# A two-layer graph network kernel: LayerNorm statistics from the adding instruction and from ScalarE, later reloads of dense tiles, another order of the last products

## The chip, the cores and the metric

The kernel runs on one core of one Trainium2 chip. The metric is the device time of one execution in microseconds, lower is better; a time given for a kernel is the median of its runs.

## The reference

The input is a matrix x of 2500 nodes by 1024 features (f32), 80,000 edges (src, dst, weight), two 1024 x 1024 weight matrices and a bias. Two residual layers follow each other, each on the ReLU of a LayerNorm without scale and shift:

```python
h = jnp.maximum(_layernorm(x, axis=-1), 0.0)
# layer 0: messages from src, weighted, summed at dst
support = jnp.matmul(h, W0)
x1 = x + segment_sum(support[src] * edge_weight[:, None], dst, 2500)
h = jnp.maximum(_layernorm(x1, axis=-1), 0.0)
# layer 1: a normalized graph convolution with self loops, row = src, col = dst
hid = jnp.einsum('nd,od->no', h, W1) + b
norm = deg_inv_sqrt[row] * deg_inv_sqrt[col]
out = x1 + segment_sum(norm[:, None] * hid[col], row, 2500)
```

The LayerNorm between them, of x1, is the one that the change touches: for every row its mean m, its variance v, and max((x1 - m) / sqrt(v + eps), 0).

## The kernel before

Nodes are cut into 20 tiles of 128 rows. The edges come sorted by dst, and tile t has TILE_BLOCKS[t] blocks of 128 edges (146, 62, 48, 41 for tiles 0 to 3, then 36 down to 10).

**First stage.** For each tile: the statistics of x, a transposed and normalized tile, its product with W0 (L282), and a store of the rows into `support` in DRAM. Beside that, edges are counted: for each block two one-hot matrices (VectorE, L446 and L448) are multiplied (L450), and VectorE adds the result to `counts[t]` (L458). For tiles 0 to 3, the "dense" ones (DENSE = 4), weighted sums are built as well (L455, L462, L466), so that their aggregation is a plain matrix product later.

**Middle stage.** The other sixteen, the "thin" tiles, are aggregated block by block in `gathered` (L587): an indirect DMA on the POOL queue brings 128 rows of `support` into `msg` (L592, eight buffers), VectorE makes a one-hot matrix `oh_r` (L596), ScalarE makes `hi`, the weighted message rounded to fp32r (L598), VectorE the remainder `lo` (L600), each with two buffers, and TensorE multiplies the one-hot matrix with both (four matmuls, L604). The dense tiles go in pairs, (3, 2) and then (1, 0), through `multiplied` (L613): for each half of the columns, 20 steps of two products `dense` x `support` (L632), whose messages come by a plain DMA on the POOL queue (L625). At the end of a half VectorE adds x (L640) and SP stores both tiles' halves to `x1_d` in DRAM (L642).

**`finish` (L552)** takes a tile on. A thin tile loads x, adds the sums from PSUM (L562, VectorE) and stores x1 to `x1_d` on SP's queue (L563). A dense tile is read back from `x1_d` on SP's queue (L557), since its halves came at different times. Then comes `normed` (L138): bn_stats on both halves and bn_aggr (VectorE, L133 and L135), the square root on ScalarE (L141), the reciprocal and the shift on VectorE (L142, L143), and the Relu with scale and shift on ScalarE (L145), which gives `hn`. `transposed` (L542) turns it on TensorE (L546) with copies by ScalarE (L547), and `second_rows` (L571) multiplies it with W1 (L577, 32 hardware matmuls per tile), adds the bias in two halves (L581, VectorE) and stores `hid` (L584, SP). `hn` and `hid` share a name and so the same two buffers of the pool `work`.

**What sets the order.** A list `plan` of 458 steps (L654 to L669) says for each step whether a dense or a thin piece is next. Beside it, the loop at L695 takes pieces of products at a `rate`, one part of a tile's preparation (`preparing`) each time that `parts` has reached 1, and as many counting groups as three planner clocks (TensorE, VectorE, ScalarE) allow: every generator yields what it takes of each (for `normed` 2.2 us of VectorE and 1.5 of ScalarE), and counting goes on until VectorE's clock has passed TensorE's (L519 to L523), or while more is left than a line that falls over the plan allows. A preparation begins only when fewer than two products are left over (L714). Tiles that still wait at the end are worked off at L732 to L737: first the preparations, then the products. The framework may move instructions of one engine against this order where its own timing model finds the engine free; `order_behind` (L274) adds an edge, without a semaphore, that keeps an instruction behind another one in that order.

**Second stage.** From L758 on, `hid` is read back, scaled and split into hi and lo (L764 to L769), and the second aggregation is 20 row tiles x 20 tiles of matmuls with the transposed counts (L794), finished by an add and a store (L782, L784). The buffers of this stage take the place of those of the middle stage, whose last user is the last product.

The two places that the change rewrites in the loop and after it:

```python
        if parts == 1 and preparing is None and len(products_left) < 2 and (waiting or stored):
            preparing = waiting.pop(0) if waiting else finish(stored.pop(0))
...
    for rest in [preparing] * (preparing is not None) + waiting:
        for _ in rest:
            pass
    for rest in products_left:
        for _ in rest:
            pass
```

Of the kernel before, what the change touches and what calls it, by code (L numbers as in the profile page):

```python
# [9 lines left out]
F32 = mybir.dt.float32  # L10
# [5 lines left out]
AF = mybir.ActivationFunctionType  # L16
ALU = mybir.AluOpType
DVE = mybir.EngineType.DVE

P = 128  # L20
# [12 lines left out]
DENSE = 4  # L33
# [14 lines left out]
def direct(  # L48
# [26 lines left out]
    nc = tc.nc  # L75
    N, D = x.shape
# [13 lines left out]
    def rows(t):  # L90
        return min(P, N - t * P)
# [17 lines left out]
    eps = keep.tile([P, 1], F32, name="eps")  # L109
# [9 lines left out]
    lay = first.enter_context(tc.tile_pool(name="lay", bufs=1))  # L119
    work = first.enter_context(tc.tile_pool(name="work", bufs=2))  # L120
# [9 lines left out]
    def moments(xt, pool):  # L130
        stats = pool.tile([P, 2, 6], F32, name="stats")
        for h in range(2):
            nc.vector.bn_stats(stats[:, h, :], xt[:, h * H:(h + 1) * H])  # L133
        mv = pool.tile([P, 2], F32, name="mv")
        nc.vector.bn_aggr(mv, stats)  # L135
        return mv

    def normed(xt, pool):  # L138
        mv = moments(xt, pool)
        rstd = pool.tile([P, 2], F32, name="rstd")  # L140
        nc.scalar.activation(rstd[:, 0:1], mv[:, 1:2], AF.Sqrt, bias=eps)  # L141
        nc.vector.reciprocal(rstd[:, 0:1], rstd[:, 0:1])  # L142
        nc.vector.scalar_tensor_tensor(rstd[:, 1:2], mv[:, 0:1], -1.0, rstd[:, 0:1], op0=ALU.mult, op1=ALU.mult)  # L143
        hn = pool.tile([P, D], F32, name="hn")
        nc.scalar.activation(hn, xt, AF.Relu, scale=rstd[:, 0:1], bias=rstd[:, 1:2])  # L145
        return hn

    def load_rows(t, pool):
        xt = pool.tile([P, D], F32, name="xt")
        if rows(t) < P:  # L150
            nc.vector.memset(xt, 0.0)
        nc.sync.dma_start(xt[:rows(t), :], x[t * P:t * P + rows(t), :])
        return xt
# [92 lines left out]
    bias = lay.tile([P, D], F32, name="bias")  # L246
# [16 lines left out]
    last_pe = None  # L263
# [3 lines left out]
    def on_pe(i):  # L267
        nonlocal last_pe
        last_pe = i
        if len(fences) >= BEHIND and fences[-BEHIND] is not None:  # L270
            order_behind(i, fences[-BEHIND])
        return i

    def order_behind(i, other):  # L274
        tc.add_manual_dep(i.ins, other.ins.name,
                          mybir.DependencyInfo(mybir.DependencyClass.NoSync, mybir.DependencyReason.SCHED_ONLY),
                          reason="order of the steps")
# [60 lines left out]
    for a in range(0, NBP, 4 * P):  # L338
# [5 lines left out]
                                       op0=ALU.max, op1=ALU.min)  # L344
# [10 lines left out]
    for t in range(NT):  # L355
# [3 lines left out]
        for a, n, m, g0 in ((a, n, g, g0), (a + n * g, int((b - a) % g > 0), (b - a) % g, g0 + n)):  # L359
            if n:  # L360
                v = first_row[:, a:a + n * m].rearrange("p (n g) -> p n g", g=m)
                nc.vector.tensor_copy(base_i[0:1, g0:g0 + n], v[0:1, :, 0])
                for q in range(1, m) if t < 2 else ():
# [9 lines left out]
                                   accum_out=placed[:, 0:1])  # L373
# [24 lines left out]
    rest = wgt_p[:, :KD]  # L398
    for i in range(2):
# [3 lines left out]
        rest = wpart[:, 2]  # L403
# [121 lines left out]
    def count_all(t):  # L525
        for queue in to_count:
            while any(g[0] == t for g in queue):
                count_next(queue)
# [13 lines left out]
    def transposed(v, into):  # L542
        for k0 in range(0, KC, 4):
            pT = psum.tile([P, 4, P], F32, name="pT")
            for k in range(4):
                nc.tensor.transpose(pT[:, k, :], v[:, (k0 + k) * P:(k0 + k + 1) * P], ident)  # L546
            nc.scalar.copy(into[:, k0:k0 + 4, :], pT)  # L547
            yield 0.7, 0.0, 0.6
# [3 lines left out]
    def finish(t, sums=None):  # L552


        if sums is None:
            xt = work.tile([P, D], F32, name="xt")
            nc.sync.dma_start(xt, x1_d[t])  # L557
            for _ in range(3):
                yield 0.0, 0.0, 0.0
        else:  # L560
            xt = load_rows(t, work)
            nc.vector.tensor_add(xt, sums.rearrange("p h d -> p (h d)"), xt)  # L562
            nc.sync.dma_start(x1_d[t], xt)  # L563
            yield 0.0, 1.25, 0.0
        hn = normed(xt, work)
        yield 0.0, 2.2, 1.5
        vT = work.tile([P, KC, P], F32, name="vT")
        yield from transposed(hn, vT)
        products_left.append(second_rows(t, vT))
# [39 lines left out]
            yield 0.92, 1.47, 1.16  # L609

    last_load = None

    def multiplied(ts):  # L613


        nonlocal last_load, pending
        for t in ts:
            count_all(t)
        for h in range(2):
            sums = psum.tile([P, 2, H], F32, name="mm")  # L620
            cols = slice(h * H, (h + 1) * H)
            for k0 in range(0, NT, 2):
                msg = gpool.tile([P, 2, H], F32, name="msg", bufs=8)
                if rows(k0 + 1) == P:
                    last_load = nc.gpsimd.dma_start(  # L625
                        msg, support[k0 * P:(k0 + 2) * P, cols].rearrange("(k p) d -> p k d", p=P))
                else:
                    for k in (k0, k0 + 1):
                        last_load = nc.gpsimd.dma_start(msg[:rows(k), k - k0], support[k * P:k * P + rows(k), cols])
                for k in (k0, k0 + 1):  # L630
                    for i, t in enumerate(ts):
                        m = nc.tensor.matmul(sums[:, i, :], dense[t][:rows(k), k, :], msg[:rows(k), k - k0],  # L632
                                             start=(k == 0), stop=(k == NT - 1))
                        if i == 0:
                            on_pe(m)
                    if k == NT - 1:
                        xt = work.tile([P, 2, H], F32, name="xt")
                        for i, t in enumerate(ts):
                            nc.sync.dma_start(xt[:, i], x[t * P:(t + 1) * P, cols])
                        nc.vector.tensor_add(xt, sums, xt)  # L640
                        for i, t in enumerate(ts):
                            nc.sync.dma_start(x1_d[t][:, cols], xt[:, i])  # L642
                        takes(v=1.25)
                        if h == 1:
                            stored.extend(ts)
                            pending += PIECES * len(ts)
                    yield 1.75, 0.0, 0.0

# [22 lines left out]
    waiting, stored, products_left = [], [], []  # L671
# [16 lines left out]
    def rows_of(tiles):  # L688
        for i in range(0, DENSE, 2):
            yield from multiplied(tiles[i:i + 2])  # L690
# [3 lines left out]
    preparing = None  # L694
    for i, is_dense in enumerate(plan):  # L695
        if stretch[i]:
            rate = min(pending - (3 if i + stretch[i] < len(plan) else 0), 14) / stretch[i]
        took = next(kinds[is_dense])
        if i == OPENING:
            for k in range(KC):  # L700
                w1_sb.append(wpool.tile([P, D], F32, name=f"w{k}"))
        if i >= OPENING and (i - OPENING) < KC:
            order_behind(nc.sync.dma_start(w1_sb[i - OPENING], w1t[(i - OPENING) * P:(i - OPENING + 1) * P, :]),
                         last_load)
        if i == OPENING + KC:
            nc.sync.dma_start(bias, b1.rearrange("(o d) -> o d", o=1).to_broadcast([P, D]))
        pieces = min(pieces + rate, 2.0)
        while pieces >= 1 and products_left:
            takes(*next(products_left[0]))
            pieces, pending = pieces - 1, pending - 1  # L710
            if pending % PIECES == 0:
                assert next(products_left.pop(0), None) is None
        parts = min(parts + 0.7, 1.0)
        if parts == 1 and preparing is None and len(products_left) < 2 and (waiting or stored):  # L714
            preparing = waiting.pop(0) if waiting else finish(stored.pop(0))
        if parts == 1 and preparing is not None:
            part = next(preparing, None)
            if part is None:
                preparing = None
            else:  # L720
                takes(*part)
                parts = 0.0
        count(*took, least=todo * (1 - 1.05 * (i + 1) / len(plan)))
# [5 lines left out]
            count_next(queue)  # L729
    store_counts(late=False)  # L730
    assert not stored
    for rest in [preparing] * (preparing is not None) + waiting:  # L732
        for _ in rest:
            pass
    for rest in products_left:
        for _ in rest:
            pass  # L737


    nc.vector.tensor_reduce(deg, total, axis=mybir.AxisListType.X, op=ALU.add)  # L740
# [17 lines left out]
    lay = ctx.enter_context(tc.tile_pool(name="lay2", bufs=1, reuse_waits="tile"))  # L758
    work = ctx.enter_context(tc.tile_pool(name="work2", bufs=2, reuse_waits="tile"))
    psum = ctx.enter_context(tc.tile_pool(name="psum2", bufs=2, space=bass.MemoryType.PSUM, reuse_waits="tile"))  # L760
    his, los = {}, {}
    for t in ORDER:
# [6 lines left out]
                                       op0=ALU.mult, op1=ALU.subtract)  # L769
# [370 lines left out]
```

## Time and profile before

| what | value |
|---|---|
| median of 3 runs | 1740.54 us (1735.30 to 1742.44) |
| the profiled execution | 1733.96 us |
| its span, first to last instruction | 1732.0 us |
| granted TensorE clock | 0.988 |
| TensorE matmul busy | 1654.1 us (96%) |
| VectorE busy | 1200.3 us (69%) |
| ScalarE busy | 907.9 us (52%) |
| HBM read and written | 282.41 MB and 54.56 MB |

The profile is one execution. Its page lists busy time by engine and the span in 40 slices; a group is all instructions of one line, engine and operation with the mean duration of one (in ns) and the idle time of the engine just before them, by what ended it. The waits list says who waited for whom, with the total, the number and the longest. The chain of waits follows the work back from the last instruction; each of its lines has start, length and what ran. The ends of matmuls are modelled, and they are pipelined, so a busy TensorE isn't one at its peak. A matmul of f32 data over 512 columns is two hardware instructions.

By stretch: until about 480 us the first stage runs, from 480 to 1346 the middle stage, and from there the second aggregation. The last counting matmuls run near 1130 us. The last dense pair is added at 1192.2 us, the last thin tile at 1316.9 us.

### The profile page before, as it was taken

The numbers are of one execution on the slowest core, as the hardware profiler recorded it, in microseconds if no ns is written. First come the engines' busy times: TensorE is split into PE (matmuls) and PEld (weight loads), VectorE is DVE, ScalarE is ACT, GpSimd is POOL, SyncE is SP. The second block draws the span as 40 slices with busy tenths as digits, with TensorE's granted clock in tenths as the row PEclk, the third lists the DMA queues.
The fourth block names the chain that finished last, engine by engine and source line by source line (L and its number), as shares of the span: only waits on it lengthen the run. The fifth ranks groups of instructions, "written<-read, shape, count | busy, mean of one in ns | idle before, by whom it ended". The sixth has DMA issues, their size and how long they took to land. (4 is left out here: it accounts for less than half of the span.)

```text
span 1732.0 us, 21214 instructions
## 1 busy us (share of the span) xinstructions
PE 1654.1 (96%) x6506; PEld 1030.8 (60%) x6506; DVE 1200.3 (69%) x3051; ACT 907.9 (52%) x1476; POOL 525.6 (30%) x501
## 2 busy tenths in 40 slices
PE   6999999999999999999999999998999899999997
PEld 2466555554445555655555555654564678888886
DVE  5788888888889999999999999996772510000000
ACT  3399999982236765665555556664553421111110
POOL 3000000000057776775555556664530000000000
PEclk9999999999999999999999999999999999999999
DMA  7512212123399999998988899898875663433320
GB/s 249 188 62 65 89 53 60 54 68 92 79 364 330 384 317 323 331 362 281 308 286 282 282 322 331 318 333 297 264 265 134 210 164 91 107 79 105 93 65 32
DMA packets 213584, 351.57 MB, mean 203 GB/s; under 512 B 115354, under 2 KB 134820, under 8 KB 213462
## 3 DMA queue, kind: packets, MB, share of 16 engines
q0 software_dynamic: 60592, 219.74, 36.2%
q1 hardware_dynamic: 152870, 130.39, 24.8%
q8 instruction: 54, 0.88, 0.2%
q14 instruction: 68, 0.56, 0.1%
HBM read 282.41 MB, written 54.56 MB: 195 GB/s over the span
## 5 line engine op out<-in xcount | busy, mean ns | idle before, releaser
L598 ACT ACTIVATE hi<-msg,wgt_p 128x1024 fp32r<-128x1024 f32 x378 | 428.6, 1149 | 280.6 <-PE mm L604 180.4
L592 POOL DMA_INDIRECT msg<-support,src_p x378 | 478.0, 1265 | 293.6 <-DVE oh_r L596 90.0
L600 DVE SCALAR_TENSOR_TENSOR lo<-msg,wgt_p,hi 128x1024 fp32r<-128x1024 f32 x378 | 480.1, 1277 | 36.7 <-ACT hi L598 21.1
L604 PE MATMUL mm<-lo,oh_r 128*128 128x512 f32 x756 | 309.8, 491 | 13.2 <-DVE lo L600 13.0
L282 PE MATMUL mm<-w,hT 128*128 128x512 f32 x640 | 318.4, 609 | 2.4 <-ACT hT L174 2.4
L577 PE MATMUL pT<-w,vT 128*128 128x512 f32 x640 | 312.4, 597 | 0.0
L604 PE MATMUL mm<-hi,oh_r 128*128 128x512 f32 x756 | 273.5, 442 | 0.7 <-ACT hi L598 0.7
L455 ACT ACTIVATE wl<-oh_low,wpart 128x128 bf16<-128x128 bf16 x891 | 262.2, 420 | 0.0
L794 PE MATMUL mm<-hi,bT 128*128 128x512 f32 (+1 forms) x800 | 247.6, 392 | 4.6 <-ACT bT L776 2.0
L794 PE MATMUL mm<-lo,bT 128*128 128x512 f32 (+1 forms) x800 | 247.7, 392 | 3.3 <-DVE lo L768 3.3
L782 DVE SCALAR_TENSOR_TENSOR rows<-mm,dis,rows 128x1024 f32<-128x1024 f32 x20 | 25.7, 1283 | 307.9 <-PE mm L794 307.8
L604 PEld LDWEIGHTS mm<-lo,oh_r 128*128 128x128 f32 x756 | 137.9, 189 | 129.3 <-DVE lo L600 51.1
L448 DVE TENSOR_SCALAR oh_key<-iota,key 128x200 bf16<-128x200 f16 (+12 forms) x675 | 194.4, 290 | 5.0 <-PE cb L462 4.9
L776 ACT CAST bT<-cT 128x2560 fp32r<-128x2560 f16 x20 | 46.6, 2335 | 261.0 <-PE mm L794 257.7
L604 PEld LDWEIGHTS mm<-hi,oh_r 128*128 128x128 f32 x756 | 139.3, 189 | 64.2 <-issue 30.2
L794 PEld LDWEIGHTS mm<-hi,bT 128*128 128x128 f32 (+1 forms) x800 | 150.4, 189 | 37.9 <-ACT hi L766 3.1
L794 PEld LDWEIGHTS mm<-lo,bT 128*128 128x128 f32 (+1 forms) x800 | 150.0, 188 | 38.3 <-DVE lo L768 7.0
L458 DVE TENSOR_TENSOR counts<-cb,counts 128x200 f32 (+13 forms) x296 | 138.5, 469 | 48.0 <-PE cb L450 41.2
L446 DVE TENSOR_SCALAR oh_low<-iota,low 128x128 bf16<-128x128 f16 x675 | 167.2, 251 | 1.4 <-ACT wl L455 1.2
L632 PE MATMUL mm<-msg,dense 128*128 128x512 f32 (+1 forms) x320 | 157.1, 601 | 10.2 <-DMA msg<-support 10.2
L577 PEld LDWEIGHTS pT<-w,vT 128*128 128x128 f32 x640 | 120.9, 191 | 72.6 <-issue 55.5
L282 PEld LDWEIGHTS mm<-w,hT 128*128 128x128 f32 x640 | 109.1, 195 | 65.4 <-issue 59.2
(144 smaller groups left out, 1177.5 us busy)
## 6 DMA issues: line engine op xcount, KB each, us to landing
msg<-support POOLq DMA_DIRECT2D x36, 512.0 KB, 6.8
xt<-in_x SPq DMA_DIRECT2D x34, 512.0 KB, 7.3
cnat<-counts SPq DMA_DIRECT2D x20, 640.0 KB, 5.4
hid_d<-hn SPq DMA_DIRECT2D x20, 512.0 KB, 6.5
rows<-hid_d SPq DMA_DIRECT2D x20, 512.0 KB, 4.4
rows<-x_d SPq DMA_DIRECT2D x20, 512.0 KB, 3.8
hT<-in_xT SPq DMA_DIRECT2D x19, 512.0 KB, 3.7
support<-row SPq DMA_DIRECT2D x19, 512.0 KB, 2.9
```

The costliest lines, as they stand in the source:

```text
L282: on_pe(nc.tensor.matmul(mm[:, h, :], vT[:, k, :], ws[k][:, h * H:(h + 1) * H], start=(k == 0), stop=(k == KC - 1)))
L446: nc.vector.tensor_scalar(oh_low, iota16[:, :P], low[:, k:k + 1], None, op0=ALU.is_equal)
L448: nc.vector.tensor_scalar(oh_key[:, :NT * w], iota16[:, :NT * w], key[:, k:k + 1], None, op0=ALU.is_equal)
L455: nc.scalar.activation(wl[:, i, :], oh_low, AF.Copy, scale=wpart[:, i, k:k + 1])
L458: nc.vector.tensor_tensor(to, cb[:, :NT * w].rearrange("p (t w) -> p t w", w=w), to, op=ALU.add)
L577: on_pe(nc.tensor.matmul(mm, vT[:, k, :], w1_sb[k][:, h * H:(h + 1) * H], start=(k == 0), stop=(k == KC - 1)))
L592: nc.gpsimd.indirect_dma_start(out=msg, out_offset=None, in_=support, in_offset=bass.IndirectOffsetOnAxis(ap=src_p[:, k:k + 1], axis=0))
L598: nc.scalar.activation(hi, msg, AF.Copy, scale=wgt_p[:, k:k + 1])
L600: nc.vector.scalar_tensor_tensor(lo, msg, wgt_p[:, k:k + 1], hi.bitcast(F32), op0=ALU.mult, op1=ALU.subtract)
L604: i = nc.tensor.matmul(sums[:, h, :], oh, v[:, h * H:(h + 1) * H], start=(j == 0 and v is hi), stop=(j == n - 1 and v is lo))
L632: m = nc.tensor.matmul(sums[:, i, :], dense[t][:rows(k), k, :], msg[:rows(k), k - k0], start=(k == 0), stop=(k == NT - 1))
L794: nc.tensor.matmul(mm[:, h, :], bT[:rows(k), k, :], v[:rows(k), h * H:(h + 1) * H], start=(k == ORDER[0] and v is his[k]), stop=(k == ORDE ...
```

## The change

In `normed`, bn_stats and bn_aggr are gone. The row sum `sum_` comes in as an argument, VectorE turns it into minus the mean, ScalarE takes Square of x1 minus the mean with its sum as accumulator output (its elements go into `hn`, which Relu overwrites later), and Sqrt takes scale 1/D. For a thin tile the row sum is the accumulator output of the add, now a scalar_tensor_tensor; for a dense tile the add at the end of each half is one scalar_tensor_tensor per tile with an accumulator output into `halves[t]`, and the two are added in `finish`. For a dense tile Square is ordered behind the last TensorE instruction written before it. The planner is told 0.4 us of VectorE and 2.7 of ScalarE for `normed`. An entry of `stored` becomes ready after four steps. At the end, products left over are worked off before the remaining preparations, and once more after them.

```diff
--- before.py
+++ after.py
@@ -135,14 +135,19 @@
         nc.vector.bn_aggr(mv, stats)
         return mv
 
-    def normed(xt, pool):
-        mv = moments(xt, pool)
+    def normed(xt, sum_, pool, behind):
+
+        hn = pool.tile([P, D], F32, name="hn")
+        mean = pool.tile([P, 2], F32, name="mean")
+        nc.vector.tensor_scalar(mean[:, 0:1], sum_, -1.0 / D, None, op0=ALU.mult)
         rstd = pool.tile([P, 2], F32, name="rstd")
-        nc.scalar.activation(rstd[:, 0:1], mv[:, 1:2], AF.Sqrt, bias=eps)
+        i = nc.scalar.activation(hn, xt, AF.Square, bias=mean[:, 0:1], accum_out=rstd[:, 1:2])
+        if behind is not None:
+            order_behind(i, behind)
+        nc.scalar.activation(rstd[:, 0:1], rstd[:, 1:2], AF.Sqrt, scale=1.0 / D, bias=eps)
         nc.vector.reciprocal(rstd[:, 0:1], rstd[:, 0:1])
-        nc.vector.scalar_tensor_tensor(rstd[:, 1:2], mv[:, 0:1], -1.0, rstd[:, 0:1], op0=ALU.mult, op1=ALU.mult)
-        hn = pool.tile([P, D], F32, name="hn")
-        nc.scalar.activation(hn, xt, AF.Relu, scale=rstd[:, 0:1], bias=rstd[:, 1:2])
+        nc.vector.tensor_mul(mean[:, 1:2], mean[:, 0:1], rstd[:, 0:1])
+        nc.scalar.activation(hn, xt, AF.Relu, scale=rstd[:, 0:1], bias=mean[:, 1:2])
         return hn
 
     def load_rows(t, pool):
@@ -555,15 +560,19 @@
         if sums is None:
             xt = work.tile([P, D], F32, name="xt")
             nc.sync.dma_start(xt, x1_d[t])
+            sum_ = work.tile([P, 1], F32, name="sum_")
+            nc.vector.tensor_add(sum_, halves[t][:, 0:1], halves[t][:, 1:2])
             for _ in range(3):
                 yield 0.0, 0.0, 0.0
         else:
             xt = load_rows(t, work)
-            nc.vector.tensor_add(xt, sums.rearrange("p h d -> p (h d)"), xt)
+            sum_ = work.tile([P, 1], F32, name="sum_")
+            nc.vector.scalar_tensor_tensor(xt, sums.rearrange("p h d -> p (h d)"), 1.0, xt,
+                                           op0=ALU.mult, op1=ALU.add, accum_out=sum_)
             nc.sync.dma_start(x1_d[t], xt)
             yield 0.0, 1.25, 0.0
-        hn = normed(xt, work)
-        yield 0.0, 2.2, 1.5
+        hn = normed(xt, sum_, work, last_pe if sums is None else None)
+        yield 0.0, 0.4, 2.7
         vT = work.tile([P, KC, P], F32, name="vT")
         yield from transposed(hn, vT)
         products_left.append(second_rows(t, vT))
@@ -609,6 +618,7 @@
             yield 0.92, 1.47, 1.16
 
     last_load = None
+    halves = {t: lay.tile([P, 2], F32, name=f"halves{t}") for t in range(DENSE)}
 
     def multiplied(ts):
 
@@ -637,12 +647,13 @@
                         xt = work.tile([P, 2, H], F32, name="xt")
                         for i, t in enumerate(ts):
                             nc.sync.dma_start(xt[:, i], x[t * P:(t + 1) * P, cols])
-                        nc.vector.tensor_add(xt, sums, xt)
                         for i, t in enumerate(ts):
+                            nc.vector.scalar_tensor_tensor(xt[:, i], sums[:, i], 1.0, xt[:, i], op0=ALU.mult,
+                                                           op1=ALU.add, accum_out=halves[t][:, h:h + 1])
                             nc.sync.dma_start(x1_d[t][:, cols], xt[:, i])
                         takes(v=1.25)
                         if h == 1:
-                            stored.extend(ts)
+                            stored.extend([4, t] for t in ts)
                             pending += PIECES * len(ts)
                     yield 1.75, 0.0, 0.0
 
@@ -711,8 +722,13 @@
             if pending % PIECES == 0:
                 assert next(products_left.pop(0), None) is None
         parts = min(parts + 0.7, 1.0)
-        if parts == 1 and preparing is None and len(products_left) < 2 and (waiting or stored):
-            preparing = waiting.pop(0) if waiting else finish(stored.pop(0))
+        for entry in stored:
+            entry[0] -= 1
+        if parts == 1 and preparing is None and len(products_left) < 2:
+            if waiting:
+                preparing = waiting.pop(0)
+            elif stored and stored[0][0] <= 0:
+                preparing = finish(stored.pop(0)[1])
         if parts == 1 and preparing is not None:
             part = next(preparing, None)
             if part is None:
@@ -729,12 +745,15 @@
             count_next(queue)
     store_counts(late=False)
     assert not stored
-    for rest in [preparing] * (preparing is not None) + waiting:
-        for _ in rest:
-            pass
-    for rest in products_left:
-        for _ in rest:
-            pass
+
+    def exhaust(generators):
+        while generators:
+            for _ in generators.pop(0):
+                pass
+
+    exhaust(products_left)
+    exhaust([preparing] * (preparing is not None) + waiting)
+    exhaust(products_left)
 
 
     nc.vector.tensor_reduce(deg, total, axis=mybir.AxisListType.X, op=ALU.add)
```

## The prediction

> **What bounds the kernel now.** I read the stretches first, then the waits, then the chain of waits at the two places where TensorE stands still, then the groups. The profiled execution took 1733.96 us, 1.96 us outside its span of 1732.0; the median of the three runs is 1740.54, so the profiled one is 6.6 us below it. Sums are made against 1733.96; the answer is carried over to the median.
>
> Busy time by stretch (length, then PE, PEld, DVE, ACT, POOL with instruction counts, clock, DMA share, GB/s):
>
> ```profile
> 560.00:1192.00 632.00, 616.20 (x2120) 368.69 (x2119) 592.98 (x1100) 384.87 (x361) 407.87 (x332) 1.00 0.91 318
> 1192.00:1207.00 15.00, 10.40 (x39) 6.22 (x37) 4.92 (x7) 6.17 (x7) 3.00 (x4) 0.99 0.91 350
> 1207.00:1317.00 110.00, 108.60 (x351) 64.48 (x352) 79.34 (x119) 56.43 (x58) 41.71 (x36) 0.97 0.66 222
> 1317.00:1346.00 29.00, 25.21 (x62) 11.44 (x60) 5.07 (x10) 8.40 (x7) 0.00 (x0) 0.94 0.64 163
> ```
>
> From 560 to 1192 TensorE and VectorE both look full (616 and 593 of 632) and the DMA engines nearly so (0.91), while ScalarE is at 61%. PE busy overstates: where nothing holds it, the chain shows four L577 or L632 matmuls in 1.72 us (0.43 each) and four of L604 in 0.93 (0.23). With 1177 of L604, 677 of L577 and L632, and some 25 us for counts and transposes, 560 to 1192 needs 271 + 291 + 25 = 587 us: about 45 us of stalls, mostly short ones. From 1207 on, counting is over and TensorE alone decides, apart from two holes.
>
> ```profile
> ACT hi L598 <- PE mm L604: 180.4, 168, 6.4
> ACT rstd L141 <- DVE mv L135: 38.1, 15, 9.7
> DVE stats L133 <- DMA xt<-x_d: 7.5, 1, 7.5
> ```
>
> ScalarE mostly waits for TensorE to free a `hi` buffer, and in LayerNorm for VectorE's moments, 2.5 us each time; VectorE waited once, for 7.5 us, for a reloaded dense tile. The chain around that wait (start, length, what):
>
> ```profile
> 1192.24 1.24 DVE xt L640
> ...
> 1193.50 6.68 DMA x_d<-xt
> ...
> 1200.32 5.92 DMA xt<-x_d
> ...
> 1207.15 1.21 DVE lo L600
> 1208.40 1.22 PE mm L604 x2
> ```
>
> The last dense pair is added, stored and read back; VectorE's queue holds that tile's statistics ahead of a ready `lo`, and TensorE stands until 1208.40. By the spacing of matmul ends this hole costs 6.6 us. The second hole is at the end of the stage:
>
> ```profile
> 1316.94 1.24 DVE xt L562
> ...
> 1321.08 1.25 ACT hn L145
> ...
> 1322.37 1.55 PE pT L546 x8
> 1323.91 21.95 PE pT L577 x48
> ```
>
> TensorE waits for tile 19's whole LayerNorm, 4.0 us by matmul ends, and only then takes 48 product matmuls, 16 of which (half of tile 18) needed nothing of it. The second aggregation begins behind the last of the 48, so both holes push the end one for one.
>
> **The change part by part.** *VectorE's work.* Durations by group:
>
> ```profile
> L133 DVE BATCH_NORM_STATS2 stats<-xt 128x6 f32<-128x512 f32 x80 | 52.2, 679 | 10.0 <-DMA xt<-x_d 7.5 <-DMA xt<-in_x 2.4
> L562 DVE TENSOR_TENSOR xt<-mm,xt 128x1024 f32<-128x1024 f32 x16 | 19.6, 1222 | 10.6 <-PE mm L604 10.4
> L782 DVE SCALAR_TENSOR_TENSOR rows<-mm,dis,rows 128x1024 f32<-128x1024 f32 x20 | 25.7, 1283 | 307.9 <-PE mm L794 307.8
> ```
>
> A thin tile now costs 1.222 + 2 x 0.679 + 0.202 (L135) + 0.156 (L142) + 0.159 (L143) = 3.10 us. Afterwards: the add as a scalar_tensor_tensor of a PSUM and an SBUF operand, as L782 (1.283); the read of its accumulator; three 128x1 operations of 0.16. What the accumulation costs is read from one instruction that has it and one of the same shape without:
>
> ```profile
> L372 DVE SCALAR_TENSOR_TENSOR inside<-row_p,inside x1: 850/850/850, 57.8 to 57.8; 128x675 f32<-128x675 f32 x1
> L372 DVE DVE_READ_ACCUMULATOR inside<-row_p,inside x1: 80/80/80, 58.6 to 58.6; 128x1 f32 x1
> L392 DVE SCALAR_TENSOR_TENSOR inside<-off,inside x1: 843/843/843, 74.1 to 74.1; 128x675 f32<-128x675 f32 x1
> ```
>
> So 0.007 + 0.08. A rule of the Trainium skill speaks against this edit: Vector Engine (DVE) Microarchitecture Reference, section "Points that are easy to get wrong", says that this form halves its throughput with two non-bf16 SBUF sources, because no port is left to read the accumulator. L372 has just that, two f32 SBUF sources and an accumulator, at the rate of L392. By the rule the twenty adds could cost about 1.1 us more each, 22 us, and the edit would save nothing; by the row it is free, and here one source is PSUM besides. I take the row: 1.283 + 0.08 + 0.48 = 1.84, a saving of 1.26 us per thin tile. A dense tile: 1.21 + 1.88 = 3.09 before; after, two half adds of 0.68 (L581, 128x512) + 0.06 + 0.09 = 0.83 each and four small operations of 0.16: 2.3, a saving of 0.8. Over all, 16 x 1.26 + 4 x 0.8 = 23 us of VectorE; before 1192 (13 thin, 2 dense) 18 us.
>
> *ScalarE's work.* Twenty Squares over 128x1024, priced as L598 (1.149, one pointer operand; L145 with two took 1.236), plus an accumulator read that no ScalarE row shows: between VectorE's 0.08 and a whole 128x1 ACTIVATE, 0.29 (L141). I take the middle; 1.3 us x 20 = 27 us. The cover is ScalarE's wait for moments (2.5 us each, of which the two statistics and the aggregate, 1.56 us, are now gone) and its 180 us of waiting for TensorE. Uncovered, each Square would delay the `hi` behind it, then `lo` and TensorE: 27 us. Below nothing it can't go, as it is added work. A table switch is the other price: ScalarE: Activation LUTs, section "Table sets: the hidden batching unit", has functions of different sets pay a load at every switch, and names relu, copy, identity and abs as present in every set, but not square. The trace has two loads of 1.283 us in all, with Sqrt, Relu and Copy alternating throughout. If Square shared no set with Sqrt, two loads per tile would add 20 x 2 x 1.28 = 51 us to ScalarE. I take none: the same page counts square with relu and identity to the functions of its tightest precision class, and the nearest row, Relu, never needed a load; the slower case below holds the other end.
>
> *New waits.* VectorE's reciprocal now stands behind Square and Sqrt, with the next `lo` and one-hots queued behind it and TensorE behind those. In the trace other VectorE work (`lo`, counts) is put between moments and reciprocal, and L142 waited 0.6 us in all twenty tiles. I take 0 to 0.5 us each. Square also takes its `hn` buffer some 3 us before Relu did; two buffers serve `hn` and `hid`. The tightest case is tile 19: `hid` of tile 17 was issued for store at 1309.9 and stores take 6.5, so it is free at 1316.4, before the new Square at about 1318.5. No cost.
>
> *The four-step delay.* Followed through the planner's loop with its numbers, the last column of each dense pair falls at plan steps 173 and 409, and its first reload at 178 and 414, already five steps behind because the slot for preparing is taken or a product is due. With the delay it is 178, 222, 414 and 427, as before: the delay moves nothing, and no DMA on SP. What does act is the order edge on Square: VectorE's two early operations no longer need the reload, and ScalarE's Square is queued behind TensorE's work of step 420, which ran near 1224 and would run near 1217, after the reload's landing at 1206.2. The 6.6 us hole closes: 6.6 us. Late next is TensorE itself (messages for those blocks landed by 1206).
>
> *Leftover products first.* By the planner the end is unchanged: half of tile 18's product and all of tile 19 left. The 16 matmuls (6.9 us) now run from 1317 to 1324, over tile 19's LayerNorm, which still takes about 5.4 us: it keeps its sum of latencies, Square in place of the statistics. The hole of 4.0 and part of the 0.6 behind it go: 4.4 us. SP's transposes of counts (14.9 us from 1319.98) move up with the rest and end before the last `hid` store.
>
> *The middle.* The planner books 1.8 us less VectorE per tile than now, and so brings the last count from step 372 forward to 336. Before that step the saved time is mostly refilled with counts, behind it VectorE is slack and TensorE bounds. Of the stalls between 560 and 1192, about 8 us are TensorE waiting for dense messages (DMA), untouched, and about 6 us lie right at LayerNorms (567, 568, 625, 686, 1113, 1152), where VectorE is relieved. I take 4 of these 6 and 1 of the rest: 5 us, between minus 5 and plus 18.
>
> Sum: 6.6 + 4.4 + 5 = 16 us. 1734 - 16 = 1718 for a profiled execution like this one; 1740.5 - 16, about 1724.5, for the median.
>
> **The rivals.**
> - *TensorE or DMA, not VectorE, bounds the middle* (share 0.91 speaks for it): the middle gives between 3 and minus 5; the holes alone, 6 to 14 us: 1727 to 1734. Chance 0.22.
> - *VectorE's relief counts in full*: 18 + 11 = 29 us: 1712. The near-equal load of TensorE speaks against. Chance 0.11.
> - *The reload hole survives*, the scheduler queueing something else behind it: 16 - 6.6 = 9.4, 1731. Chance 0.05.
> - *Slower: Square becomes the wait.* It sits in ScalarE's queue ahead of a `hi` for which VectorE and TensorE have nothing else left; 1.3 us x 20 = 27 and 0.3 us of reciprocal wait x 20 = 6, less the 11 of the holes and nothing for the middle: plus 22, 1762. It decides from about 0.55 us per tile on the path (where it eats the 11). Against it: ScalarE idles 39% of the middle. With table loads it would be more. Chance 0.07.
>
> **How the numbers follow.** Likeliest (0.55): 16 us, own range 10 to 22, 1718 to 1731. The range to hold 8 in 10 takes in the full relief and most of the first rival: 1711 to 1736. About 0.5% (8.7 us, the border is 1731.8) is what a measurement of this kernel can tell from no change: faster by more, 0.50 of the likeliest case, 0.11, 0.06 of the first rival and 0.03 of the third, 0.70; within, 0.23; slower, 0.07.
>
> **What would show it.** VectorE's busy time falls by about 23 us and ScalarE's rises by about 27; no wait of VectorE for x_d over 1 us; no 6 us wait of TensorE for `lo`; the product matmuls run on behind the last sums, and the transposes of tile 19 after them. Wrong would be: a reciprocal or `lo` waiting over 10 us in all for Square, table loads above two, or a middle stretch not shorter than now.

## The result, and the profile after

The changed kernel takes 1717.54 us (median of 4 runs, 1713.82 to 1719.61) against 1739.14 of the kernel before in the same measurement: ratio 0.9878, interval 0.9856 to 0.9901, some 21 us. Forecast were 1724.5 us and a gain of 16. The profiled execution took 1716.88 us, its span 1714.9.

To place the gain I use one sum throughout. For a stretch of the trace, "stall" is its length less what its matmuls take when nothing holds them, by the spacing of their ends: 0.429 us for L282, L577 and L632, 0.229 for L604, 0.227 for L794, 0.109 for the small transpositions (L546 and those of the first stage), 0.086 for a count. The first stage ends where the first dense matmul starts, each stretch of tiles with the last matmul of a thin tile, and the second aggregation starts with its first matmul:

| stretch | before: length, stall | after: length, stall |
|---|---|---|
| first stage | 479.6, 78.9 | 478.2, 77.5 |
| tiles 4 to 6 | 200.9, 30.4 | 200.2, 31.4 |
| tiles 7 to 12 | 334.3, 20.4 | 338.5, 21.5 |
| tiles 13 to 16 | 171.4, 9.7 | 166.2, 5.7 |
| tile 17 (last dense pair's add lies in it) | 58.3, 9.1 | 49.6, 0.4 |
| tiles 18 and 19 | 72.4, 0.3 | 72.6, 0.5 |
| last thin sums to the second aggregation | 30.0, 6.6 | 24.8, 1.4 |
| second aggregation | 385.1, 21.9 | 384.8, 21.6 |

Two stretches carry the gain that these two executions show: tile 17 with 8.7 us and the end of the middle stage with 5.2. The middle before them seems to give only 1.7; that is a matter of which execution of the kernel before was profiled, as the last run below shows.

The busy time by stretch, of the changed kernel (columns as in the prediction; the stretches are moved along with the work):

```profile
560.00:1189.00 629.00, 616.08 (x2121) 366.05 (x2120) 577.41 (x1095) 402.46 (x392) 403.73 (x331) 1.00 0.92 320
1189.00:1205.00 16.00, 16.00 (x58) 9.93 (x57) 11.40 (x21) 8.10 (x9) 6.68 (x7) 1.00 0.98 366
1205.00:1305.00 100.00, 100.00 (x333) 59.48 (x332) 69.70 (x102) 58.41 (x64) 39.28 (x33) 1.00 0.69 238
1305.00:1330.00 25.00, 23.79 (x64) 10.94 (x62) 4.73 (x13) 9.87 (x10) 0.00 (x0) 1.00 0.74 189
```

TensorE is busy for all of the 16 us behind the last dense add, where it had 10.40 of 15. VectorE has 577 us to do up to there in place of 593, ScalarE 402 in place of 385. TensorE's wait for `lo` before, and then the waits of the changed kernel that answer to those shown of before (waiter, waited for, total us, times, longest):

```profile
PE mm L604 <- DVE lo L600: 13.0, 19, 6.0
```

```profile
ACT hi L607 <- PE mm L613: 168.7, 143, 6.4
ACT hn L144 <- DVE mean L142: 28.3, 13, 7.8
PE mm L613 <- DVE lo L609: 7.7, 21, 0.7
```

VectorE no longer waits for the reload of a dense tile at all. ScalarE's wait for the moments (38.1 us at the square root) is now one for the mean (28.3, at Square), and TensorE's longest wait for `lo` is 0.7 us, down from 6.0. The chain of waits where the first hole was:

```profile
1183.95 5.15 PE mm L642 x12
1189.10 0.44 PE pT L551 x4
1189.54 1.72 PE pT L586 x4
1191.26 0.92 PE mm L613 x4
1192.18 0.44 PE pT L551 x4
1192.62 0.93 PE mm L613 x4
```

It doesn't leave TensorE: the store and the reload are gone from it. The end of the stage:

```profile
1305.26 8.60 PE pT L586 x20
1313.86 0.02 issue
1313.88 0.70 DVE hn L590
1314.58 0.04 issue
1314.63 0.66 PE pT L551 x4
1315.28 13.75 PE pT L586 x32
```

The 20 product matmuls left of tile 18 run from the last thin sums on, over tile 19's LayerNorm. Of the hole 0.6 us is left, by the spacing of matmul ends: the second transposition waits until VectorE has emptied one of the two `pT` buffers. The new instructions' durations, from the lists of three lines (minimum, median, maximum in ns):

```profile
L570 DVE SCALAR_TENSOR_TENSOR xt<-mm,xt x16: 1209/1224/1225, 560.6 to 1305.3; 128x1024 f32<-128x1024 f32 x16
L570 DVE DVE_READ_ACCUMULATOR xt<-mm,xt x16: 76/83/88, 561.8 to 1306.4; 128x1 f32 x16
L651 DVE SCALAR_TENSOR_TENSOR xt<-mm,xt x8: 678/685/692, 563.2 to 1189.8; 128x512 f32<-128x512 f32 x8
L144 ACT ACTIVATE hn<-xt,mean x20: 1130/1148/1158, 563.1 to 1306.8; 128x1024 f32<-128x1024 f32 x20
L144 ACT ACTIVATION_READ_ACCUMULATOR hn<-xt,mean x20: 184/187/188, 564.2 to 1307.8; 128x1 f32 x20
```

The accumulating add takes what the plain one did (1.222 us), and its read 0.08. Square takes 1.15, its read 0.19. These are durations of single instructions; a read begins before the instruction ahead of it has ended (by 0.075 us on VectorE and 0.094 on ScalarE, medians of this trace), so sums of durations are larger than busy time. There are still two table loads in all.

### The profile page after: what moved, and what is told of

It reads as the page before. It is cut to its first block, busy times and chain, and to the rows that moved or that the text cites. A ratio compares the mean times of both kernels' runs of the same rounds, so it can differ in the third digit from the quotient of the medians.

```text
span 1714.9 us, 21228 instructions
## 1 busy us (share of the span) xinstructions
PE 1646.6 (96%) x6506; PEld 1023.9 (60%) x6506; DVE 1181.0 (69%) x3043; ACT 930.3 (54%) x1516; POOL 521.0 (30%) x501
## 5 line engine op out<-in xcount | busy, mean ns | idle before, releaser
L609 DVE SCALAR_TENSOR_TENSOR lo<-msg,wgt_p,hi 128x1024 fp32r<-128x1024 f32 x378 | 480.6, 1280 | 36.4 <-ACT hi L607 21.4
L287 PE MATMUL mm<-w,hT 128*128 128x512 f32 x640 | 314.8, 603 | 2.4 <-ACT hT L179 2.4
L586 PE MATMUL pT<-w,vT 128*128 128x512 f32 x640 | 308.8, 592 | 0.0
L613 PE MATMUL mm<-lo,oh_r 128*128 128x512 f32 x756 | 295.1, 471 | 8.1 <-DVE lo L609 7.7
L613 PE MATMUL mm<-hi,oh_r 128*128 128x512 f32 x756 | 279.2, 450 | 0.5 <-ACT hi L607 0.5
```

The lines of the kernel that those rows point to most:

```text
L287: on_pe(nc.tensor.matmul(mm[:, h, :], vT[:, k, :], ws[k][:, h * H:(h + 1) * H], start=(k == 0), stop=(k == KC - 1)))
L586: on_pe(nc.tensor.matmul(mm, vT[:, k, :], w1_sb[k][:, h * H:(h + 1) * H], start=(k == 0), stop=(k == KC - 1)))
L609: nc.vector.scalar_tensor_tensor(lo, msg, wgt_p[:, k:k + 1], hi.bitcast(F32), op0=ALU.mult, op1=ALU.subtract)
L613: i = nc.tensor.matmul(sums[:, h, :], oh, v[:, h * H:(h + 1) * H], start=(j == 0 and v is hi), stop=(j == n - 1 and v is lo))
```

## The experiments

Theory after the result: two holes of TensorE closed, one because nothing that waits for a reload stands early in VectorE's queue, one because the left-over products now cover the last LayerNorm; the rest is VectorE's relief. In doubt were the part of the order edge, what the relief is worth, what Square costs, and whether the planner's new numbers help or hurt. The kernel before was timed beside every group of runs: 1737.9, 1738.3 and 1738.5 us.

**Without the delay.**

```diff
-                            stored.extend([4, t] for t in ts)
+                            stored.extend([0, t] for t in ts)
```

> The changed kernel without the four-step delay: an entry of `stored` is ready at once. Theory (the delay moves nothing, since by the planner's steps the reloads fall at 178, 222, 414 and 427 either way): 1717.5 us, within 3 us of the changed kernel, and so a measure of how far two executions of one order of work lie apart. Rival (the delay is what closes the reload hole at 1192 to 1208): about 6 to 9 us slower than the changed kernel, 1724 to 1727, with TensorE standing for 6 us at the last dense pair.

Measured: 1717.4 us (ratio to before 0.9890, 0.9867 to 0.9913). The order of the instructions on all five engines is the same as with the delay, so the delay does nothing, and the run tells the scatter: 1712 to 1723 over the ten executions of this one order of work, with a median of 1717.5. The runs below are set against that median.

**The old order at the end.**

```diff
-    exhaust(products_left)
     exhaust([preparing] * (preparing is not None) + waiting)
     exhaust(products_left)
```

> The changed kernel with the old order at the end: first the last preparation, then all left-over products. Theory: TensorE again waits for tile 19's LayerNorm, which keeps its length of about 5.4 us, so the stretch from the last thin add to the first matmul of the second aggregation grows from 24.8 to about 30 us: 5 us slower than the changed kernel, 1722.5. Rival (the new LayerNorm is shorter by itself, and that is what filled the hole): within 1.5 us of the changed kernel.

Measured: 1724.15 us (0.9925, 0.9903 to 0.9948), 6.7 us slower than the changed kernel. The chain of waits at the end shows the hole again:

```profile
1310.09 1.24 DVE xt L570 x2
...
1311.54 1.25 ACT hn L144 x2
...
1313.53 1.25 ACT hn L150
1314.78 0.04 issue
1314.82 1.97 PE pT L551 x8
1316.79 21.49 PE pT L586 x48
```

From the last sums to the second aggregation it has 29.3 us with 5.9 of stall (24.8 and 1.4 with the new order): 4.5 us lie there; the other 2 are within the scatter of executions. The new LayerNorm is a little shorter (the add's start to Relu's end 4.7 us, before 5.4), but not short enough to matter without the order.

**Without the order edge.**

```diff
-        hn = normed(xt, sum_, work, last_pe if sums is None else None)
+        hn = normed(xt, sum_, work, None)
```

> The changed kernel without the order edge on a dense tile's Square. Theory of the prediction (the edge keeps the wait for the reload out of the way): the hole at the last dense pair comes back, on ScalarE's queue in place of VectorE's, 4 to 9 us slower than the changed kernel, 1722 to 1727. Rival (taking the statistics off VectorE is enough, as no VectorE instruction that is queued early needs the reloaded tile any more): within 2 us of the changed kernel, no stall of TensorE over 1 us between the adds of tiles 16 and 17.

Measured: 1719.94 us (0.9895, 0.9876 to 0.9915), 2.4 us slower than the changed kernel, with overlapping intervals. The stall of tile 17 is 0.4 us, as with the edge. The reloads, from the list of their line, and Square of the first dense tile in ScalarE's timeline, without the edge:

```profile
L562 SPq DMA_DIRECT2D xt<-x_d x4: 319/320/320, 755.0 to 1202.1; - x4
DMA to landing us min/median/max: 7.5/7.7/7.9
```

```profile
1216.48 1.13 ACT L144 ACTIVATE hn<-xt,mean 128x1024 f32<-128x1024 f32 x1
```

The reload was issued by 1202.1 and took at most 7.9 us, so Square comes 6 us after it has landed, without waiting; in this order it has moved by a single `hi` against the changed kernel. The edge isn't what closes the hole. The framework put Square late by itself; what a Square placed early in ScalarE's queue would cost, no run shows.

**The edge alone, in the kernel before.**

```diff
         for h in range(2):
-            nc.vector.bn_stats(stats[:, h, :], xt[:, h * H:(h + 1) * H])
+            i = nc.vector.bn_stats(stats[:, h, :], xt[:, h * H:(h + 1) * H])
+            if behind is not None:
+                order_behind(i, behind)
...
-        hn = normed(xt, work)
+        hn = normed(xt, work, last_pe if sums is None else None)
```

> The kernel before with one addition: a dense tile's two statistics instructions on VectorE are ordered behind the last TensorE instruction written before them. Everything else is as before. If the hole is a matter of where the wait for the reload stands in VectorE's queue: the stall between the adds of tiles 16 and 17 falls from 8.8 us to under 1, and the kernel is 7 to 9 us faster than before, about 1731. Rival (the hole needs VectorE's work taken away, or it only moves on in the queue): within 3 us of before, 1739.

Measured: 1731.85 us (0.9968, 0.9953 to 0.9982), 6 us faster than before (3 to 8), a little less than expected. Tile 17's stall is 0.5 us. The dense pair's add and the first statistics of the reloaded tile, in VectorE's timeline:

```profile
1197.17 1.23 DVE L642 TENSOR_TENSOR xt<-mm,xt 128x1024 f32<-128x1024 f32 x1 [0.93 <-PE mm L634]
...
1223.87 1.28 DVE L133 BATCH_NORM_STATS2 stats<-xt 128x6 f32<-128x512 f32 x2
```

The statistics now come 27 us after the add and wait for nothing. So the hole was the place of a waiting instruction in VectorE's queue; either cure, the edge or the removal of the statistics, closes it. (In this profile tile 8, where the first dense pair is prepared, has 7.4 us of stall against 4.4; whether the edge causes that was not settled, as the repeat of the kernel before has 6.0 there.)

**The planner's old numbers in the changed kernel.**

```diff
-        yield 0.0, 0.4, 2.7
+        yield 0.0, 2.2, 1.5
```

> The changed kernel with the planner's old numbers for `normed` (2.2 us of VectorE and 1.5 of ScalarE). By the planner the last count goes back from step 336 to 372, about 1130 us in place of 1068. Theory (the 3 us that the middle stage gained behind 1060 us come from having no counts there any more): the stalls between the adds of tiles 12 and 16 rise from 5.7 us to about 9, and the kernel is 3 us slower than the changed one, 1720.5. Rival (they come from VectorE's shorter LayerNorm itself): within 1.5 us of the changed kernel, those stalls under 7.

Measured: 1714.56 us (0.9872, 0.9853 to 0.9891): not slower but 3 us faster. Both expectations missed. The last count comes at 1123 us, and the late tiles' stalls rise as expected (7.9 from 5.7), but those of tiles 7 to 12 fall more (17.6 from 21.5).

**The planner's new numbers in the kernel before** (the same line, the other way).

> The kernel before with the planner's new numbers for `normed` (0.4 us of VectorE and 2.7 of ScalarE) and nothing else: the planner believes in a relief that isn't there and counts earlier. If the place of the counts alone makes the middle's gain: stalls between the adds of tiles 12 and 16 fall from 9.7 us to about 6, and the kernel is 3 us faster than before, 1735. If VectorE is what bounds tiles 6 to 12: their stalls (20 us before) rise by 5 to 10 us and the kernel is 2 to 7 us slower than before, 1740 to 1745.

Measured: 1740.5 us over 22 runs, ratio 1.0009, 0.9998 to 1.0020. Tiles 7 to 12 stall 28.3 us, tiles 13 to 16 8.2: without the relief, counting earlier moves work to where VectorE has no room, and the place of the counts alone gains nothing.

**Square twice.**

```diff
-        i = nc.scalar.activation(hn, xt, AF.Square, bias=mean[:, 0:1], accum_out=rstd[:, 1:2])
-        if behind is not None:
-            order_behind(i, behind)
+        for _ in range(2):
+            i = nc.scalar.activation(hn, xt, AF.Square, bias=mean[:, 0:1], accum_out=rstd[:, 1:2])
+            if behind is not None:
+                order_behind(i, behind)
```

> The changed kernel with Square and its accumulator read done twice for each tile (the second overwrites the same values), 20 x 1.33 = 27 us more of ScalarE. Theory (ScalarE's queue has room at the LayerNorms, where it otherwise waits): at most 3 us slower than the changed kernel, under 1721. Rival (Square stands in front of a needed `hi`): 10 to 27 us slower, 1728 to 1745.

Measured: 1721.82 us (0.9904, 0.9886 to 0.9921), 4.3 us slower, with intervals that overlap a little: between the two expectations, nearer the first. ScalarE's busy time rose from 930.3 to 951.7 us, by 21.4 (27 by the sum of durations), so a fifth of the added busy time reached the end. Square is covered for the most part, not wholly.

**The old statistics kept on VectorE beside the new ones.**

```diff
+        if behind is None:
+            moments(xt, pool)
         hn = pool.tile([P, D], F32, name="hn")
```

> The changed kernel with bn_stats and bn_aggr of the sixteen thin tiles left in on VectorE beside the new statistics, their result unused: 16 x 1.56 = 25 us of VectorE come back (13 of the tiles, 20 us, before the last dense add), while the reload, Square and the end stay as in the change. Theory (the two holes are the gain, and VectorE's relief is worth little): 1 to 6 us slower than the changed kernel, 1718 to 1724. Rival (VectorE bounds the middle): 15 to 20 us slower, 1733 to 1738.

Measured: 1730.76 us (0.9959, 0.9945 to 0.9974), 13.2 us slower: between the two expectations. The holes stay closed (tile 17 0.3 us, end 1.4), and tiles 7 to 12 stall 30.1 us. VectorE's busy time is 1200.7 us, 19.7 more than in the changed kernel (25 by the sum of durations). This work is worth more than half of itself here; that the relief is worth little, the first expectation, falls.

**The same with the planner's old numbers.** Both edits together, the statistics kept and `yield 0.0, 2.2, 1.5`.

> Both at once: bn_stats and bn_aggr of the thin tiles left in on VectorE (unused, 25 us), and the planner's old numbers, so that counts are placed as in the kernel before; both holes stay closed. It is the kernel before with its holes closed and nothing relieved. Theory now (VectorE does bound part of the middle, and the relief is worth about half of its 25 us wherever the counts lie): 12 us slower than the changed kernel with old planner numbers, about 1726.5. Rival (the relief seemed dear only because the counts were crowded into tiles 7 to 12; with the old numbers there is room): 1718 to 1721.

Measured: 1724.24 us (0.9929, 0.9904 to 0.9955), 9 us slower than the changed kernel with old numbers, nearer the first expectation than the second. VectorE is busy for 1199.5 us, as in the kernel before. Against the run before, the old numbers save 6.5 us: with the statistics kept, the earlier counts cost that much, three times what they seem to cost without them.

**Counts later still.** `yield 0.0, 3.4, 1.5` in the changed kernel.

> The changed kernel with planner numbers for `normed` that overstate VectorE (3.4 us, ScalarE 1.5): the last count goes to plan step 384. If crowding counts into tiles 7 to 12 is what cost the 3 us between the two settings so far, spreading them further gives 1712 to 1715, with stalls of tiles 7 to 12 under 17.6 us. Rival (the late tiles fill up in turn): 1716 to 1720, stalls of tiles 13 to 16 over 8 us.

Measured: 1715.31 us (0.9868, 0.9845 to 0.9892). Its stalls (18.7 in tiles 7 to 12, 8.3 in 13 to 16) are close to those of the old numbers, and neither expectation is met in full: nothing more was gained in this direction.

**The old numbers again.**

> The changed kernel with the planner's old numbers once more, unchanged, beside the others on one chip: if its 3 us over the changed kernel are real, its median lies at 1713 to 1716 again; if they were scatter between executions, at 1717 to 1719.

Measured: 1715.5 us (0.9873, 0.9852 to 0.9893). Over both runs of it the mean of 9 executions is 1715.4, and over the 10 of the changed kernel and its twin without the delay 1717.5. The 2 us have the same sign in all four comparisons (this one, its first run, the kernel before, the kept statistics), but each pair of intervals overlaps; I take them as likely, not as settled.

**The kernel before again.**

> The kernel before once more, for a second profiled execution. The first took 1733.96 us, while the median of its 27 runs is 1738.3. If that gap lies in the middle stage, the stalls from 480 us to the add of tile 16 (60.5 us in the first) are about 64 to 65 here in an execution near the median, and the middle's gain of the change is 4 us larger than the two first profiles show. If it is spread over the whole span, every stretch is longer by some 0.2%.

Measured: 1738.04 us, ratio 0.9994. Its profiled execution took 1741.73 us, and the first one 1733.96: 7.8 us apart. The busy time of the same stretch in the repeat:

```profile
560.00:1192.00 632.00, 612.87 (x2101) 366.79 (x2100) 586.70 (x1087) 381.77 (x358) 400.50 (x327) 0.99 0.91 315
```

In the same 632 us it got through 19 matmuls and 13 VectorE instructions fewer than the first profile. From 480 us to tile 16 it has 68.9 us of stall, the first 60.5; the first stage is 2.3 us shorter in the repeat, the end of the middle stage 1.3 longer, the rest the same to 0.4. So one program's middle stage differs by 8 us between executions, and the first profile shows one of its quick ones. Half way between the two, at an execution of about the median, the middle has 710.9 us against 704.9 after: a gain of 6. The changed kernel's middle varies as well: in the same order of work it takes 704.1 us in the profile without the delay and 710.0 in the one with the old end (both executions slower than the one profiled first), so this 6 is good to some 3 us only.

## Why the prediction was right, and where not

By medians the whole is now a chain of runs: before 1738.3; both holes closed, VectorE as busy as before and Square already on ScalarE, counts as before 1724.2 (minus 14.1, by the interval 8 to 17); VectorE relieved 1715.4 (minus 9); the planner's new numbers 1717.5 (plus 2).

*The reload hole.* Put at 6.6 us, the one wait between 1202 and 1208; it gave 8.7. The step counted the long wait and not the shorter stalls around it in the same stretch (its total was 9.1). The edge alone, by medians of whole executions, gave 6. The prediction's reason was wrong in one link: it said that what acts is the order edge. Without the edge the hole stays closed, and the edge alone closes it in the kernel before; removing the statistics from VectorE suffices, since what is left there (the halves' sum and the mean) needs no reload and the reciprocal comes after Square, late enough.

*The four-step delay.* Nothing, as worked out: the order of instructions is the same.

*Left-over products first.* Put at 4.4 us; the stretch gave 5.2 in the profile. The run with the old order puts 4.5 of them down to the order, as forecast, and is 6.7 us slower in all. The LayerNorm was taken as 5.4 us long and is 4.7.

*VectorE's work.* Put at 23 us less, busy time fell by 19.3. The 23 is a sum of durations, and by durations the LayerNorm's own instructions did fall by 25 us: the thin add was priced from L782 (1.283), which has a scalar from a pointer, and with the constant 1.0 it takes 1.221. But durations overlap, and other VectorE instructions take longer than before, 10 us by durations (the one-hot matrix of a message has a mean of 0.295 us in place of 0.288); why, no run shows. The rule that the prediction set against this edit (Trainium skill, Vector Engine (DVE) Microarchitecture Reference, section "Points that are easy to get wrong") is about two SBUF sources that aren't bf16. The adds have one source in PSUM, so they don't try it; half the rate would have been, as an estimate, 2.4 us each, twice the plain add's 1.222. The row L372, which the prediction followed, decided rightly.

*ScalarE.* Put at 27 us of added work, with no cost on the path. By durations that is what was added, 20 x (1.145 + 0.187) = 27, but busy time rose by 22.4 only (907.9 to 930.3), since neighbours overlap. One tile's Square, its read and the square root in ScalarE's timeline:

```profile
1214.56 1.14 ACT L144 ACTIVATE hn<-xt,mean 128x1024 f32<-128x1024 f32 x1
1215.60 0.19 ACT L144 ACTIVATION_READ_ACCUMULATOR hn<-xt,mean 128x1 f32 x1
1215.82 0.29 ACT L147 ACTIVATE rstd<-rstd,eps 128x1 f32<-128x1 f32 x1
```

On the path the second Square cost 4.3, so the first probably costs a few us as well, where the prediction had none; no run takes it out alone. The slower rival needed 0.55 us per tile on the path; 4.3 / 20 is 0.2. The reciprocal's wait for ScalarE is 3.5 us in twenty tiles (profile after), within the 0 to 10 allowed. No table load came: Square, Sqrt, Relu and Copy alternate with the same two loads as before.

*The middle.* Put at 5 us net, it is about 6. The parts were mis-sized and in part made up for each other, which was luck: the relief was taken as nearly refilled by counts, and is worth 9 us at old planner numbers and 13 at the new; the new numbers, which the prediction saw bringing the counts forward, seem to cost some 2 us instead of nothing. A likely reason, which no run shows by itself, is that they book 1.8 us of relief per tile where 1.26 were expected from the durations, and so crowd the counts into tiles 7 to 12. The sum 16 was short of 21 by 2 in the first hole, 1 in the second, 1 in the middle; what is left is within the scatter.

## What to carry to other kernels

Here one VectorE instruction that waited 7.5 us for a round trip through DRAM held a ready `lo` behind it, and with it TensorE for 6.6 us: look in the trace for such a single long wait for a DMA, and either order the waiter later or take its work off that engine; both closed the hole here. TensorE and VectorE shared the load of this middle stage closely (616 and 593 of 632 us), and taking 18 to 20 us of busy time off VectorE was worth 9 to 13; in another kernel this can be measured in the same way, by putting the old work back beside the new form. One profile is one execution: before a difference of some us in a long stage is explained, profile the same kernel twice.

## What was not expected of the hardware

A scalar_tensor_tensor over 128x1024 with a constant scalar takes 1.221 us with an accumulator output, a tensor_tensor of the same operands 1.222; with the scalar from a pointer (L782) it is 1.283. ScalarE's read of its accumulator takes 0.187 us, VectorE's 0.083, and both begin before the instruction ahead of them has ended. And the same program, with TensorE's clock at 0.987 to 0.988 in both, had 8 us more stall in its middle stage in one execution than in another; what causes it, perhaps the landing of messages at a DMA share of 0.9, was not tried.
